# Attention scores in four column tiles of 32, masked in four pieces, with the value projection's scaling moved ahead of the third chunk's product

## The chip, the cores and the metric

The kernel runs on one core of a Trainium2 chip. The metric is the time on the device in microseconds, from several executions of which the median counts. One execution was profiled; all rows shown here are from that one.

A core has five engines that run side by side, each through its own queue in order: TensorE (PE, with its weight loads listed apart as PEld), VectorE (DVE), ScalarE (ACT), GpSimd (POOL) and SyncE (SP), which here only issues transfers.

## The reference

A layer of chunked linear attention, followed by a gated feed-forward layer, each with a residual and a layer normalization. Tokens are 4 x 2048 with 256 features. Cut to what matters:

```python
CHUNK = 32
Q, K, V = x @ W_q.T, x @ W_k.T, x @ W_v.T
diff = pos[:, None] - pos[None, :]                      # positions within a chunk of 32
mask = where(diff >= 0, decay ** diff, 0)
S = einsum('bncd,bnkd->bnck', Qc, Kc) * mask            # scores, 32 x 32 in each chunk
O = einsum('bnck,bnkd->bncd', S, Vc)
x = layernorm(x + (sigmoid(x @ W_g.T) * O) @ W_o.T + x)
gate = x @ (w_gate * SCALE).T                           # 768 hidden features
up = x @ (w_up * SCALE).T
x = layernorm(x + (silu(gate) * up) @ (w_down * SCALE).T)
```

Scores exist only inside a chunk of 32 tokens. Nothing passes from one chunk to the next.

## The kernel before

The 8192 tokens are worked through in 16 blocks of 512 (`TB`), each in four groups of 128 (`NG`). A token's features lie either along the partitions (`xT`, `yT`, `hT`) or along the free dimension (`x`, `v`, `h`, `r`). Query and key weights are multiplied into one matrix m beforehand, so that the scores of a block are products of xT with yT = m xT.

**Scores.** `attn_scores` takes a group of 128 tokens in two halves of 64 (`PAIR`, two chunks). Each half is a matmul with 64 stationary columns (tokens of xT) and 64 moving ones (of yT), over two slices of 128 features; every fp32 matmul is two instructions on PE. The result `ps`, 128 x 256 numbers, holds for each pair of chunks also the products between the two chunks, which are not wanted. One DVE multiply (L655) with `mask`, a constant tile of the same shape that is zero outside the chunks, writes `sT`. The tile `mask` is made at the start by four DVE copies (L274) from `chunk_mask`, a tile of 128 x 32 that holds the decay powers.

**Values.** `value_products` (L670) multiplies sT with v in 64 x 64 tiles, four at a time, into two banks `po`, and DVE makes `goT` of them with the gate `sg`.

**Split products.** The projections y (L494), gate g (L494), v and o (L516) are each made of three products of lower-precision parts: `hi`, `lo` and `gap`. `three` issues kinds hi and lo into two banks and lets ACT scale each bank (L535); the function that it returns issues the third kind, gap, and the bank's last use. The gap product therefore waits for ACT's scaling.

**Feed-forward, up.** `ffn_up` takes one of six chunks of 128 hidden features at a time: eight matmuls into banks `fg` and `fu` (L839), ACT's silu `s` (L848), DVE's product `u` (L859), ACT's rounding `u_hi` (L864) and POOL's remainder `u_lo` (L865). With `held=True` it returns a function `multiply` that issues u, u_hi and u_lo later. `ffn_down` is L710.

**The loop.** Iteration b of the main loop does the feed-forward of block b, the attention of block n = b + 2 and the projections of block m = b + 3. In program order: normalize h of block b + 1 (ACT, L428); up chunk 0; up chunk 1; move h of b + 1 (four DVE transposes into `sq`, L791, and 16 transfers on SP's queue into `hT`, L798); scores of block n; load xT of m + 1; up chunk 2; first two kinds of v for m with ACT's scaling; up chunk 3; the gap kind of v, normalization and store of a finished block; values of n; y of m and up chunks 4 and 5; split of hT (L815, L816); gate of m and output projection of n, with residual h and its statistics (L750, L340, L341); ACT's roots (L349); down. In the first iteration (b = 0) h of block 1 is normalized and moved only after the scores; the last one (b = 13) has no block m left and takes the scores after up chunk 0. Scores of blocks 0 and 1 are made ahead of the loop, those of block 1 between two residuals of block 0 (`beside`).

The order on PE, ACT and mostly DVE is the program's: `in_turn` and `in_steady_turn` pin an instruction to its place on its engine. What isn't pinned (POOL's remainders, transfers) may be placed elsewhere.

The PSUM has eight banks that all these products share. A further function, `wide_group`, treats weights of more than 8 bits; its branch isn't taken with these inputs.

Of the kernel before, what the change touches and what calls it, by code (L numbers as in the profile page):

```python
# [47 lines left out]
F32 = mybir.dt.float32  # L48
# [4 lines left out]
ALU = mybir.AluOpType  # L53

P = 128
CHUNK = 32
PAIR = 2 * CHUNK
SQ = 32
TB = 512
NG = TB // P  # L60
# [16 lines left out]
def kernel(  # L77
# [15 lines left out]
    nc = tc.nc  # L93
    NT, D = x.shape
    H = ffn_gT.shape[1]
    KD = D // P
    KH = H // P
    NB = NT // TB
# [15 lines left out]
    def in_turn(ins):  # L114
        tc.keep_in_program_order(ins)

    def bank(name):
        return psum.tile([P, TB], F32, tag="ps", name=name)
# [9 lines left out]
    def load_xT(b, start=None, pieces=1):  # L128
        xt = xin.tile([P, KD, TB], F32, tag="xT", name=f"xT_{b}")
        src = xT[:, span(b, start)].rearrange("(k p) t -> p k t", p=P)  # L130
        n = KD // pieces
        for k in range(0, KD, n):
            queue(start).dma_start(xt[:, k : k + n, :], src[:, k : k + n, :])
        return xt
# [106 lines left out]
    for i in range(CHUNK.bit_length() - 1):  # L241
# [10 lines left out]
        in_turn(nc.vector.tensor_copy(bit, bit_int))  # L252
        in_turn(nc.vector.tensor_scalar(factor, bit, -1.0, 1.0, ALU.mult, ALU.add))
        bits.append((bit, factor))
    mask = const.tile([P, NG, PAIR], F32, tag="mask", name="mask")
    nc.vector.memset(mask, 0.0)

    def make_mask():
        in_turn(nc.scalar.activation(decay, decay, AF.Sigmoid))
        power = decay  # L260
        for i, (bit, factor) in enumerate(bits):
            in_turn(
                nc.vector.scalar_tensor_tensor(factor, bit, power, factor, ALU.mult, ALU.add)
            )
            in_turn(nc.vector.tensor_tensor(chunk_mask, chunk_mask, factor, ALU.mult))
            if i < len(bits) - 1:
                square = const.tile([P, 1], F32, tag=f"power_{i}", name=f"power_{i}")
                in_turn(nc.vector.tensor_tensor(square, power, power, ALU.mult))
                power = square
        for g in range(P // CHUNK):  # L270
            rows = slice(g * CHUNK, (g + 1) * CHUNK)
            at = g * CHUNK % PAIR
            in_turn(
                nc.vector.tensor_copy(  # L274
                    mask[rows, :, at : at + CHUNK],
                    chunk_mask[rows, :].unsqueeze(1).to_broadcast([CHUNK, NG, CHUNK]),
                )
            )

    def integers(w, w_int, name):  # L280

# [46 lines left out]
    def in_steady_turn(ins):  # L328
        if steady:
            tc.keep_in_program_order(ins)  # L330
# [231 lines left out]
    def split_v(b, x_parts):  # L562
        v = work.tile([P, NG, D], F32, tag="v", name=f"v_{b}")
        per = TB // D

        def finish(i, pb):
            in_turn(nc.scalar.copy(flat(v, slice(i * per, (i + 1) * per)), pb))

        return v, three(f"v_{b}", token_major(w_parts["wv"], x_parts), finish)
# [67 lines left out]

    def attn_scores(b, yT):
        xt = xTs.pop(b)
        halves = [slice(i * PAIR, (i + 1) * PAIR) for i in range(P // PAIR)]  # L640
        ps = bank(f"ps_{b}")[:, : NG * PAIR].rearrange("p (g c) -> p g c", c=PAIR)
        for g in range(NG):
            for fc in range(KD):
                for rows in halves:
                    tokens = slice(g * P + rows.start, g * P + rows.stop)
                    product = nc.tensor.matmul(  # L646
                        ps[rows, g, :],
                        lhsT=xt[:, fc, tokens],
                        rhs=yT[:, fc, tokens],
                        start=(fc == 0),  # L650
                        stop=(fc == KD - 1),
                    )
                    in_turn(product)
        sT = work.tile([P, NG, PAIR], F32, tag="sT", name=f"sT_{b}")
        in_steady_turn(nc.vector.tensor_tensor(sT, ps, mask, ALU.mult))  # L655
        return sT

    def by_pairs(t):
        return t.rearrange("p k (g r c) -> p (k g) r c", g=NG, c=PAIR)
# [382 lines left out]
    def up_now(b, hT, uT, hc):  # L1042
        ffn_up(b, hT, uT, range(hc, hc + 1))

    for b in range(NB - 2):
        n = b + 2
        m = b + 3
        more = m < NB
        xns[n] = load_xn(n)
        hT = hTs.pop(b)  # L1050
        uT = [], []
        yT, v, sg = ahead
        if b:
            normalize(hs[b + 1], *scales_h)
        up_now(b, hT, uT, 0)
        if not more:
            sT = attn_scores(n, yT)
        up_now(b, hT, uT, 1)
        if b:
            moving = move_h(b + 1, hs[b + 1])  # L1060
        if more:
            sT = attn_scores(n, yT)
        if b == 0:
            normalize(hs[b + 1], *scales_h)
            moving = move_h(b + 1, hs[b + 1])
        if m + 1 < NB:
            xTs[m + 1] = load_xT(m + 1)
        up_now(b, hT, uT, 2)
        if more:
            v_next, v_rest = split_v(m, x_parts)  # L1070
            up_now(b, hT, uT, 3)
            v_rest()
            if scales_out is not None:
                normalize(r_before, *scales_out)
                store(b - 2, r_before)
        goT = attn_values(n, sT, v, sg)
        if b == 0:
            look_up(range(4, n_pieces))
            cast_fd(0)
        if b == 1:  # L1080
            count = count_wide()
            n_wide_early = const.tile([1, 1], I32, tag="n_wide_early", name="n_wide_early")
            nc.vector.tensor_copy(n_wide_early, count)
        go_parts, go_gaps = token_parts(goT, f"go_{n}")
        if more:
            y_next, y_rest = split_y(m, x_parts)
        else:
            up_now(b, hT, uT, 3)
            normalize(r_before, *scales_out)
            store(b - 2, r_before)  # L1090
        up_now(b, hT, uT, 4)
        go_gaps()
        up_now(b, hT, uT, 5)
        if b == 0:
            cast_fd(1)
        elif more:
            hTs[b + 1] = split_h(b + 1, moving)
        r_before = r_out
        if more:
            y_rest()  # L1100
            sg_next, g_rest = split_gate(m, x_parts)
            hs[n], out_rest = split_out(n, go_parts)
            g_rest()
            mv_h = out_rest()
            if b == 0:
                hTs[b + 1] = split_h(b + 1, moving)
            ahead = y_next, v_next, sg_next
            if m + 1 < NB:
                x_parts, x_gaps = token_parts(xTs[m + 1], f"x_{m + 1}")
            std_h = root_in_turn(mv_h, of_h, f"h_{b}")  # L1110
            if b:
                mv_before, std_before = mv_out, root_in_turn(mv_out, of_out, f"out_{b}")
            back_to_silu()

            def between():
                scales = scale_and_shift(mv_h, std_h, of_h, f"h_{b}")
                if m + 1 < NB:
                    x_gaps()
                return scales

            r_out, mv_out, scales_h = ffn_down(b, uT, hs.pop(b), between)
            if b:
                scales_out = scale_and_shift(mv_before, std_before, of_out, f"out_{b}")
        else:
            hs[n], out_rest = split_out(n, go_parts)
            hTs[b + 1] = split_h(b + 1, moving)
            scales_out = iterated_scale_and_shift(mv_out, of_out, f"out_{b}")
            normalize(r_before, *scales_out)
            store(b - 1, r_before)

            def amid():
                return iterated_scale_and_shift(out_rest(), (HALF, 1.0), f"h_{n}")

            r_out, mv_out, scales_h = ffn_down(
                b, uT, hs.pop(b), chunkwise=True, amid=amid
            )
            normalize(hs[n], *scales_h)
            scales_out = iterated_scale_and_shift(mv_out, of_out, f"out_{b + 1}")
# [164 lines left out]
    def wide_group(start, weights):  # L1303
# [11 lines left out]
        def products(pb, pairs):  # L1315
            for i, (lhsT, rhs) in enumerate(pairs):
                nc.tensor.matmul(
                    pb, lhsT=lhsT, rhs=rhs, start=(i == 0), stop=(i == len(pairs) - 1)
                )
            return pb  # L1320
# [25 lines left out]
            bank("pv_w")[:, :D], [(xt[:, ec, :], given["wv"][:, ec, :]) for ec in range(KD)]  # L1346
        )
        nc.vector.tensor_copy(v, pv)
        sT = work.tile([P, NG, PAIR], F32, tag="sT", name="sT_w")
        ps = bank("ps_w")[:, :PAIR]  # L1350
        for i in range(P // PAIR):
            rows = slice(i * PAIR, (i + 1) * PAIR)
            products(ps[rows, :], [(xt[:, fc, rows], yT[:, fc, rows]) for fc in range(KD)])
        nc.vector.tensor_tensor(sT[:, 0, :], ps, mask[:, 0, :], ALU.mult)
        banks = [
            bank(f"po_w_{i}")[:, :P].rearrange("p (n c) -> p n c", c=PAIR)
            for i in range(P // PAIR)
# [130 lines left out]
```

## Time and profile before

| | |
|---|---|
| time, median of 3 executions | 506.77 us (506.67 to 506.98) |
| the profiled execution's time | 507.07 us |
| its span, first to last instruction | 505.5 us |
| PE busy | 493.7 us, 98% |
| ACT, DVE, POOL busy | 373.1, 301.1 and 291.4 us |
| granted TensorE clock | 0.997 of full speed |
| ps (L646) | 512 matmul instructions, 16 groups of 1.08 us |
| sT (L655) | 16 DVE multiplies, median 385 ns |
| mask (L274) | 4 DVE copies, 1,218 to 1,259 ns |

A row of the profile names the line and engine, then the operation, then output and inputs by the program's tile names. Times within the span are counted from the first instruction. A row of a timeline begins with start and duration in us; in square brackets stands how long the engine stood idle before, and what ended that. A row of the waits reads: engine, tile and line that waited, what it waited for, then the total in us, how often, and the longest. Busy shares are averages: an engine at 60% can still be the one that a stage waits for.

### The profile page before, as it was taken

Reading aid. Unit: us, or ns where it says so; the run is one execution under the profiler, and the core shown is the slowest. Engines: PE = TensorE matmul, PEld = TensorE weight load, DVE = VectorE, ACT = ScalarE, POOL = GpSimd, SP = SyncE. Lnnn points to the kernel's source line nnn. Section 1 sums busy time; section 2 is a strip of 40 time slices with the busy share of each in tenths; the row PEclk is TensorE's granted clock in tenths of the full one; section 3 lists DMA queues with packets and bytes.
Section 4 is the critical chain, followed back from the end, with each engine's and each line's share of the span. In section 5 each row is a group of like instructions: output and inputs, shape, how many; then the busy total and the mean of one; then the engine's idle time right before and its main releaser. Section 6 shows DMA issues by size and latency. Waiting matters only on the chain.

```text
span 505.5 us, 11205 instructions
## 1 busy us (share of the span) xinstructions
PE 493.7 (98%) x4248; PEld 387.0 (77%) x4248; DVE 301.1 (60%) x709; ACT 373.1 (74%) x701; POOL 291.4 (58%) x322
## 2 busy tenths in 40 slices
PE   9999889999999999999999999999999999999995
PEld 5787667787777878777787877778787787867684
DVE  4887567564564647547464664747547463656654
ACT  5867777687768777686787868777786877766845
POOL 2745546654746557465564846557474655567664
PEclk9999999999999999999999999999999999999998
DMA  8721202112222122222212312122222211103111
GB/s 264 236 83 44 66 22 83 44 43 69 65 83 79 43 77 91 61 67 84 70 58 67 99 56 74 50 76 86 64 64 85 83 43 33 54 15 107 34 36 65
DMA packets 43320, 36.93 MB, mean 73 GB/s; under 512 B 4864, under 2 KB 39168, under 8 KB 43264
## 3 DMA queue, kind: packets, MB, share of 16 engines
q1 hardware_dynamic: 42144, 35.28, 23.4%
q10 hardware_dynamic: 1120, 0.92, 0.6%
q8 instruction: 34, 0.56, 0.5%
q14 instruction: 22, 0.18, 0.1%
HBM read 20.45 MB, written 8.39 MB: 57 GB/s over the span
## 4 chain that ended last, share of the span: by engine, by line
PE 69%; ACT 5%; DVE 4%; POOL 2%; SPq 2%; issue 2%; DMA 1%; DVEq 0%; ACTq 0%; POOLq 0%
PE fg L839 14%; PE fu L839 13%; PE fdn L710 12%; PE p_y L494 6%; PE p_g L494 6%; PE p_o L516 6%; PE p_v L516 6%; PE po L670 2%; PE ps L646 2%; DVE u L859 2%; SPq L798 2%; PE fdn L913 1%; ACT s L848 1%; ACT h L428 1%; ACT u_hi L864 1%
## 5 line engine op out<-in xcount | busy, mean ns | idle before, releaser
L865 POOL TENSOR_TENSOR u_lo<-u,u_hi 128x512 f16<-128x512 f32 (+1 forms) x98 | 128.9, 1317 | 94.1 <-ACT u_hi L864 94.1
L859 DVE SCALAR_TENSOR_TENSOR u<-fu,s 128x512 f32<-128x512 f32 (+1 forms) x98 | 66.4, 678 | 123.7 <-ACT s L848 98.3
L864 ACT CAST u_hi<-u 128x512 fp32r<-128x512 f32 (+1 forms) x98 | 59.9, 612 | 78.9 <-DVE u L859 78.8
L839 PE MATMUL fg<-hT_hi,fg_hi 128*128 128x512 f32 (+1 forms) x196 | 71.1, 444 | 0.0
L848 ACT ACTIVATE s<-fg 128x512 f32<-128x512 f32 (+1 forms) x98 | 56.8, 581 | 5.7 <-PE fg L839 5.5
L839 PE MATMUL fu<-hT_hi,fu_hi 128*128 128x512 f32 (+1 forms) x196 | 60.6, 390 | 0.0
L839 PE MATMUL fg<-hT_lo,fg_lo 128*128 128x512 f16 (+1 forms) x196 | 58.3, 378 | 0.0
L839 PE MATMUL fu<-hT_lo,fu_lo 128*128 128x512 f16 (+1 forms) x196 | 57.5, 375 | 0.0
L475 POOL TENSOR_TENSOR go_lo<-goT,go_hi 128x512 fp32r<-128x512 f32 x30 | 38.9, 1315 | 26.5 <-ACT go_hi L474 26.5
L475 POOL TENSOR_TENSOR x_lo<-xT,x_hi 128x512 fp32r<-128x512 f32 x30 | 38.3, 1299 | 23.8 <-ACT x_hi L474 23.8
L710 PE MATMUL fdn<-fd_hi,u_hi 128*128 128x256 f32 x312 | 44.8, 285 | 0.0
L750 DVE TENSOR_TENSOR h<-p_o,x 128x512 f32<-128x512 f32 x30 | 19.4, 686 | 41.9 <-PE p_o L516 37.6
L839 PEld LDWEIGHTS fu<-hT_hi,fu_hi 128*128 128x128 f32 x196 | 36.6, 188 | 8.4
L839 PEld LDWEIGHTS fg<-hT_hi,fg_hi 128*128 128x128 f32 x196 | 34.8, 189 | 9.4
L710 PEld LDWEIGHTS fdn<-fd_hi,u_hi 128*128 128x128 f32 x312 | 39.0, 188 | 0.3
L428 ACT ACTIVATE h<-h,shift_h,scale_h 128x256 f32<-128x256 f32 x52 | 27.0, 590 | 16.4 <-POOL shift_h L391 16.4
L710 PE MATMUL fdn<-fd_lo,u_lo 128*128 128x256 f16 x312 | 38.6, 274 | 0.0
L816 POOL TENSOR_TENSOR hT_lo<-hT,hT_hi 128x512 f16<-128x512 f32 x28 | 35.4, 1285 | 3.8 <-ACT hT_hi L815 3.7
L839 PEld LDWEIGHTS <-fu_lo 128*128 128x128 f16 x196 | 19.2, 98 | 22.3 <-issue 0.3
L710 PEld LDWEIGHTS <-u_lo 128*128 128x128 f16 x312 | 28.4, 98 | 3.9
L688 DVE SCALAR_TENSOR_TENSOR goT<-sg,po 128x512 f32<-128x512 f32 x32 | 20.6, 684 | 16.1 <-PE po L670 16.1
L839 PEld LDWEIGHTS <-fg_lo 128*128 128x128 f16 x196 | 14.0, 98 | 20.9 <-issue 12.9
(175 smaller groups left out, 1056.9 us busy)
## 6 DMA issues: line engine op xcount, KB each, us to landing
x<-in_x_dram SPq DMA_DIRECT2D x16, 512.0 KB, 3.9
xT<-in_xT_dram SPq DMA_DIRECT2D x15, 512.0 KB, 3.7
hT<-sq SPq DMA_DIRECT2D x224, 32.0 KB, 1.9
out_dram<-r SPq DMA_DIRECT2D x13, 512.0 KB, 3.1
out_dram<-r SPq DMA_DIRECT2D x7, 128.0 KB, 1.7
fg_int<-in_ffn_gT_dram SPq DMA_DIRECT2D x3, 256.0 KB, 7.8
fu_int<-in_ffn_uT_dram SPq DMA_DIRECT2D x3, 256.0 KB, 7.1
fd_int<-in_ffn_dT_dram SPq DMA_DIRECT2D x3, 256.0 KB, 5.9
```

The lines of the kernel that those rows point to most:

```text
L428: nc.scalar.activation(r[:, g, :], r[:, g, :], AF.Identity, bias=shift[:, g : g + 1], scale=scale[:, g : g + 1],)
L475: in_turn(nc.gpsimd.tensor_tensor(lo[:, k, :], t[:, k, :], whole, ALU.subtract))
L494: nc.tensor.matmul(pb, lhsT=a[kind][:, k, i * P : (i + 1) * P], rhs=b[kind][:, k, :], start=kind + k == 0, stop=True, skip_group_check=True,)
L516: nc.tensor.matmul(pb[:, j * D : (j + 1) * D], lhsT=b[kind][:, k, g * P : (g + 1) * P], rhs=a[kind][:, k, :], start=kind + k + j == 0, sto ...
L688: nc.vector.scalar_tensor_tensor(by_pairs(goT)[:, :, r, :], by_pairs(sg)[:, :, r, :], 1.0, po, ALU.add, ALU.mult)
L710: product = nc.tensor.matmul(pb[:, j * D : (j + 1) * D], lhsT=part[:, g * P : (g + 1) * P], rhs=w, start=(i == 0), stop=(i == len(terms) - 1),
L816: nc.gpsimd.tensor_tensor(in_order[1], whole, in_order[0].bitcast(F32), ALU.subtract)
L839: product = nc.tensor.matmul(pb, lhsT=w[kind][:, dc, hc * P : (hc + 1) * P], rhs=hT[kind][:, dc, cols], start=(kind == kinds[0] and dc == ...
L848: in_turn(nc.scalar.activation(s, pg, AF.Silu, scale=SCALE / H_UP))
L859: nc.vector.scalar_tensor_tensor(u, pu, U_UP / H_UP, s, ALU.mult, ALU.mult)
L864: in_steady_turn(nc.scalar.copy(hi, u))
L865: nc.gpsimd.tensor_tensor(lo, u, hi.bitcast(F32), ALU.subtract)
```

## The change

1. Scores are made chunk by chunk: four matmuls of 32 stationary columns and 32 moving ones, each in a column tile of its own (`tile_position`), so that only the wanted 32 x 32 products exist. `ps` is half as wide.
2. `mask` and its four copies go. Two constant tiles `sTs` are set to zero once on POOL and used in turn; each block multiplies its four chunks' rows with `chunk_mask` into the places of the tile that belong to them (four DVE instructions of 32 partitions x 128 elements). The rest stays zero.
3. In the loop, up chunk 2 is called with `held=True`, and its `multiply` stands behind the first two kinds of v, whose scalings on ACT thereby come ahead of u and u_hi of that chunk.
4. In the first iteration, normalizing and moving h of block 1 stand behind that `multiply`; the load of xT stands ahead of it.

```diff
-    mask = const.tile([P, NG, PAIR], F32, tag="mask", name="mask")
-    nc.vector.memset(mask, 0.0)
...
-        for g in range(P // CHUNK):
-            rows = slice(g * CHUNK, (g + 1) * CHUNK)
-            at = g * CHUNK % PAIR
-            in_turn(
-                nc.vector.tensor_copy(
-                    mask[rows, :, at : at + CHUNK],
-                    chunk_mask[rows, :].unsqueeze(1).to_broadcast([CHUNK, NG, CHUNK]),
-                )
-            )
+
+    sTs = [const.tile([P, NG, PAIR], F32, tag=f"sT_{i}", name=f"sT_{i}") for i in range(2)]
+    for sT in sTs:
+        nc.gpsimd.memset(sT, 0.0)
...
     def attn_scores(b, yT):
         xt = xTs.pop(b)
-        halves = [slice(i * PAIR, (i + 1) * PAIR) for i in range(P // PAIR)]
-        ps = bank(f"ps_{b}")[:, : NG * PAIR].rearrange("p (g c) -> p g c", c=PAIR)
+        ps = bank(f"ps_{b}")[:, : NG * CHUNK].rearrange("p (g c) -> p g c", c=CHUNK)
         for g in range(NG):
...
-        sT = work.tile([P, NG, PAIR], F32, tag="sT", name=f"sT_{b}")
-        in_steady_turn(nc.vector.tensor_tensor(sT, ps, mask, ALU.mult))
-        return sT
+            score_products(ps[:, g, :], xt[:, :, g * P :], yT[:, :, g * P :], in_turn)
+        sTs.append(sTs.pop(0))
+        masked(sTs[-1], ps, range(NG), in_steady_turn)
+        return sTs[-1]
+
+    chunks = [slice(i * CHUNK, (i + 1) * CHUNK) for i in range(P // CHUNK)]
+
+    def score_products(ps, xt, yT, order):
+        for fc in range(KD):
+            for chunk in chunks:
+                product = nc.tensor.matmul(
+                    ps[chunk, :],
+                    lhsT=xt[:, fc, chunk],
+                    rhs=yT[:, fc, chunk],
+                    start=(fc == 0),
+                    stop=(fc == KD - 1),
+                    tile_position=(0, chunk.start),
+                )
+                order(product)
+
+    def masked(sT, ps, groups, order):
+        for i, chunk in enumerate(chunks):
+            at = i * CHUNK % PAIR
+            order(
+                nc.vector.tensor_tensor(
+                    sT[chunk, groups.start : groups.stop, at : at + CHUNK],
+                    ps[chunk],
+                    chunk_mask[chunk, :].unsqueeze(1).to_broadcast([CHUNK, len(groups), CHUNK]),
+                    ALU.mult,
+                )
+            )
...
         if more:
             sT = attn_scores(n, yT)
+        if m + 1 < NB:
+            xTs[m + 1] = load_xT(m + 1)
+        multiply = ffn_up(b, hT, uT, range(2, 3), held=True)
+        if more:
+            v_next, v_rest = split_v(m, x_parts)
+        multiply()
         if b == 0:
             normalize(hs[b + 1], *scales_h)
             moving = move_h(b + 1, hs[b + 1])
-        if m + 1 < NB:
-            xTs[m + 1] = load_xT(m + 1)
-        up_now(b, hT, uT, 2)
         if more:
-            v_next, v_rest = split_v(m, x_parts)
             up_now(b, hT, uT, 3)
```

The branch for wide weights uses the same two functions; it isn't taken here.

## The prediction

> **What bounds the kernel now.** I read the page first (busy shares and the chain that ended last), then the chain in order of time, then the timelines of PE, ACT and DVE over one block of the steady loop.
>
> ```profile
> span 505.5 us, 11205 instructions
> PE 493.7 (98%) x4248; PEld 387.0 (77%) x4248; DVE 301.1 (60%) x709; ACT 373.1 (74%) x701; POOL 291.4 (58%) x322
> ...
> 205.49 1.08 PE ps L646 x32
> ...
> 235.57 1.08 PE ps L646 x32
> ```
>
> PE is busy 98% of the span, and from 145 to 444 us the chain runs on PE alone, with a period of 30.08 us (235.57 − 205.49). Each block holds one group of scores of 1.08 us. That looks like a plain PE bound, but the list of waits says otherwise:
>
> ```profile
> PEld p_g L494 <- ACT p_g L535: 4.2, 14, 1.5
> PEld p_o L516 <- ACT p_o L535: 2.2, 12, 0.2
> PE p_v L516 <- ACT p_v L535: 1.6, 1, 1.6
> ```
>
> In every block the weight loads of the last products of gate and output (third kind, "gap") wait for ACT's scaling of their banks. In the block at 205 the second scaling of p_o ends at 225.72 and its product starts at 225.87, 0.14 later; in the block at 114, where PE stood visibly idle at 134.07, that distance is also 0.14 (135.47 to 135.61). So PE and a second loop are level to some 0.02 us. The second loop: ACT normalizes h (202.80), s and u of chunks 0 and 1, DVE's four transposes, the masking, u of chunk 2, then ACT almost back to back to the scaling of p_o, PE's last p_o products, DVE's residual and statistics, ACT's roots, POOL's shift, and the next h at 232.88.
>
> ```profile
> 207.98 1.42 DVE L791 STREAM_TRANSPOSE sq<-h 128x256 f32<-128x256 f32 x4
> 209.32 0.39 DVE L655 TENSOR_TENSOR sT<-ps,mask 128x256 f32<-128x256 f32 x1
> 209.63 0.68 DVE L859 SCALAR_TENSOR_TENSOR u<-fu,s 128x512 f32<-128x512 f32 x1
> ...
> 210.34 0.62 ACT L864 CAST u_hi<-u 128x512 fp32r<-128x512 f32 x1 [1.12 <-DVE u L859]
> 210.86 1.06 ACT L535 ACTIVATE p_v<-p_v 128x512 f32<-128x512 f32 x2
> 211.90 0.60 ACT L848 ACTIVATE s<-fg 128x512 f32<-128x512 f32 x1
> ```
>
> Here ACT stands 1.12 us for u of the third chunk, with the scaling of p_v queued behind it. Both sides of the change touch this place.
>
> **What the skill says.** The Trainium skill, "TensorE: Matmul & The Clock Gate", section on packing small matmuls: matmuls of different tiles run at once, starting about 4 ns apart. The records of single matmuls agree in kind: the two 64-column tiles of ps start 7 ns apart and the pair repeats every 58 ns; po's four 64x64 tiles also start 7 ns apart and repeat every 58. The same page states a start-to-start floor of about 25 ns for small matmuls; po's 64 in 1.09 us (17 ns each) show that it can hold within one tile only. "TensorEngine Tiling (Array Packing)", key properties: changing the tiling mode drains TensorE; here the next full matmul starts 0.15 us after the last of ps. "VectorE: DVE Perf Modes", section on two Vector instructions with no wait between them: an instruction that starts in another quadrant of partitions is held until all earlier ones have finished. The four copies of L274 (32 partitions each) fit: each starts 14 ns after the end of the one before, while the transposes overlap by 78.
>
> **The change, part by part.**
>
> *PE, scores.* 64 matmuls of 32 columns in four tiles replace 32 of 64 in two: 16 rounds either way. A round is 58 ns; its streaming part follows from L599 (512 columns, 592 ns) and L620 (256 columns, 379): 0.83 ns a column, 53 for 64, 27 for 32. The new round is 32 ns, and issuing four pairs takes 4 x 7 = 28, just under it. Saved 16 x 26 = 0.42 us, group 1.08 to 0.66. Four streams at once on all 128 rows are not in this trace; bounds: nothing saved (rounds stay at 58), or 0.49 (issue alone). A loss would need 4 tiles to run one after the other, which po's four speak against. I take 0.42.
>
> *DVE, masking.* One multiply (385 ns, 416 unpipelined) becomes four of 32x128 in four quadrants. The PSUM read of nine numbers at L319 takes 148 ns, so 128 elements at one a cycle (the same page: 0.96 GHz, one a cycle for fp32 from PSUM) give about 272; from the 256-element row, 385 − 133 = 252 pipelined. The first starts pipelined with the transposes at 209.32, the others and u are held: u of chunk 2 starts near 209.32 + 0.25 + 3 x 0.29 = 210.45 instead of 209.63. Upper bound: L274's 1,234 ns a piece. Those copies keep step with POOL's 1.3 us operations beside them, whereas L655 took 390 ns under POOL's u_lo (208.80 to 210.10); so I keep 0.29, range 0.17 (overlapped) to 0.40.
>
> *ACT, order.* The scaling of p_v no longer stands behind u. s of chunk 2 ends at 209.22, p_v's first bank is ready by then with PE 0.42 earlier, the second is scaled 210.09 to 210.63, u is done at 210.45 + 0.69 = 211.14, u_hi starts 211.18, and s of chunk 3 at 211.70 instead of 211.90. The second loop is 0.20 shorter, PE's 0.42 shorter; the smaller counts: **0.20 a block, ten blocks (145 to 444 us), 2.0 us**. With pieces of 0.17 it is PE's 0.42; at 0.33 it is nothing.
>
> *First block of the loop (50 us).* Here h is normalized in front of chunk 2, and PE pays:
>
> ```profile
> 54.15 2.08 ACT L428 ACTIVATE h<-h,term_h,y_h 128x256 f32<-128x256 f32 x4
> ...
> 58.05 1.06 ACT L535 ACTIVATE p_v<-p_v 128x512 f32<-128x512 f32 x2
> ...
> 58.68 1.22 PE L516 MATMUL p_v<-wv_gap,x_gap 128*128 128x256 f32 x8 [1.62 <-ACT p_v L535]
> ```
>
> Now normalizing follows the scaling and u, so that idle goes. But ACT does the same work up to the gate scaling (72.0), where PE waits 1.3 us again. ACT gains only idle time: s 54.15, p_v 54.65 and 55.14, u_hi 55.65, h 56.15, s of chunk 3 at 58.1 instead of 59.04. Gain 0.94. The moves of h (four transposes, 16 DMAs on SP of 0.64 us) start 2.0 us later, their last landing goes from 68.7 to 70.8, still ahead of its reader at 74.9. The load of xT that now precedes them was issued ahead of them already (51.45).
>
> *Second block (84 us).* Its p_v wait (0.24) goes and the scores give 0.42; ACT is ahead of PE here by 0.9 in the gate: 0.66. *Third (114 us):* ACT waits 0.71 for h's transfer, one of whose pieces landed late (132.14). If that recurs nothing is gained, if not some 0.9: I take 0.45. *Last (444 us):* ACT waits 0.25 for chunk 1 behind the scores: 0.25.
>
> *Start.* Two score groups stand ahead of the loop, 0.84 on PE. The second is masked between residuals (DVE 34.15 to 34.57) and po starts at 34.85. With DVE 0.42 earlier and 1.15 of pieces, sT is ready at about 34.9, so PE waits what it gained: −0.1 in all. The removed mask copies (4.98 us at 11.63) and memset end ahead of yT, whose products PE finishes at 16.8: a few tenths at most, none of it counted. The two memsets on POOL fall in its idle 4.1 us before 6.29.
>
> Sum against the profiled execution: 0.94 − 0.1 + 0.66 + 0.45 + 2.0 + 0.25 = 4.2 of a span of 505.5 us. That execution took 507.07, 0.3 above the median 506.77; from the median: **502.5**.
>
> **Rivals.** *DVE is cheap* (pieces 0.17, not held): PE's 0.42 counts in ten blocks, 4.2, with 0.9 in the third; total 6.8, **500.0**. Against it are L274's gaps. *No saving on PE* (four streams share what two had): ten blocks 0, first 0.84, second 0.24, third 0.2; 1.3 in all, **505.5**. Nothing in this trace excludes it. *Masking is the bound, slower:* DVE between transposes and u of chunk 2. Above 0.33 us a piece the loop is longer than before, above about 0.40 the loss (3 us) exceeds all gains by over 1 us. At 0.46: u at 211.16, s at 212.41, +0.51 a block, 5.1 less 1.3 gained elsewhere, **510.5**; at L274's 1.25 it would be near 545. For it: the only row of this shape. Against: 385 ns for double the elements under the same POOL load. *Even:* 0.35 to 0.40 a piece, **506.5**.
>
> **Numbers.** Forecast 0.62, cheap DVE 0.13, no PE saving 0.11 (0.07 of it faster by more than 0.2%, 0.04 not), even 0.05, slower 0.09. A difference under 0.2% (1.0 us) is about what a measurement of this kernel can't tell from none. Faster 0.82, same 0.09, slower 0.09. The forecast's own range is 501 to 504; with the cheap-DVE case and the one without PE saving 499.8 to 505.7, leaving out the slow case and half of the even one.
>
> **What would show it.** Group of ps: x64 in some 0.66 us (right), 1.08 (rival two). sT: four pieces of about 0.27 us, each starting after the end of the one before. In steady blocks p_v scaled ahead of u_hi, ACT's idle before u_hi of chunk 2 gone, and a visible PE wait of about 0.2 us at the gate's or output's last products. At 58.7 no PE wait, at 72 a longer one. At 34 us a new wait of po for sT. A period of 29.9 us: 30.1 or more would make the loop's step wrong, 29.65 the DVE price.

## The result, and the profile after

The changed kernel took 502.51 us (median of 4 executions, 502.30 to 503.24), the kernel before 506.87 beside it (4 executions, 506.67 to 506.98): a ratio of 0.9917, interval 0.9900 to 0.9934. It is faster by 4.4 us. The prediction was 502.5.

The head of the page after and the chain of waits in order of time (start, duration, what):

```profile
span 500.8 us, 12278 instructions
PE 489.9 (98%) x4760; PEld 381.8 (76%) x4760; DVE 308.0 (61%) x752; ACT 373.4 (75%) x701; POOL 291.6 (58%) x324
```

```profile
201.60 0.69 PE ps L646 x50
...
231.53 0.69 PE ps L646 x50
```

The group of scores went from 1.08 to 0.69 us, although it is now 64 instructions. The period is 29.93 (231.53 − 201.60), where it was 30.08. PE is as busy as before, 98%: the busy share could not have told that the loop changed.

The list of waits (engine, tile and line that waited, releaser, total us, times, longest):

```profile
PEld p_g L486 <- ACT p_g L527: 6.3, 23, 1.7
PEld p_o L508 <- ACT p_o L527: 2.3, 12, 0.2
PE p_g L486 <- ACT p_g L527: 2.1, 3, 1.5
```

The visible wait of p_v (1.6 us before) is not in the list any more. The weight loads of the gate's last product wait longer than before (6.3 us against 4.2): PE now reaches that place too early. Why is in the timelines of DVE and ACT at the same place in the block (start, duration; idle before and its releaser in brackets):

```profile
204.09 1.42 DVE L803 STREAM_TRANSPOSE sq<-h 128x256 f32<-128x256 f32 x4
205.43 1.17 DVE L662 TENSOR_TENSOR sT<-ps,chunk_mask 32x128 f32<-32x128 f32 x4
206.63 0.69 DVE L871 SCALAR_TENSOR_TENSOR u<-fu,s 128x512 f32<-128x512 f32 x1
```

```profile
205.28 0.58 ACT L527 ACTIVATE p_v<-p_v 128x512 f32<-128x512 f32 x1
206.22 0.58 ACT L527 ACTIVATE p_v<-p_v 128x512 f32<-128x512 f32 x1 [0.36 <-PE p_v L508]
207.35 0.62 ACT L876 CAST u_hi<-u 128x512 fp32r<-128x512 f32 x1 [0.55 <-DVE u L871]
207.88 0.59 ACT L860 ACTIVATE s<-fg 128x512 f32<-128x512 f32 x1
```

Masking takes 1.17 us instead of 0.39, and u begins 2.54 us behind the first transpose (206.63 − 204.09) instead of 1.65 (209.63 − 207.98): 0.89 later. ACT used that time for p_v's scaling, but still stood 0.55 us for u. The silu s of the fourth chunk follows the start of h's normalization by 8.97 us (198.91 to 207.88); before it was 9.10 (202.80 to 211.90). Those 0.13 us are the gain of an undisturbed block.

### The profile page after: what moved, and what is told of

It reads as the page before. It is cut to its first block, busy times and chain, and to the rows that moved or that the text cites. A ratio compares the mean times of both kernels' runs of the same rounds, so it can differ in the third digit from the quotient of the medians.

```text
span 500.8 us, 12278 instructions
## 1 busy us (share of the span) xinstructions
PE 489.9 (98%) x4760; PEld 381.8 (76%) x4760; DVE 308.0 (61%) x752; ACT 373.4 (75%) x701; POOL 291.6 (58%) x324
## 4 chain that ended last, share of the span: by engine, by line
PE 81%; ACT 8%; DVE 7%; issue 2%; POOL 1%; DVEq 0%; ACTq 0%; POOLq 0%
PE fg L851 15%; PE fu L851 14%; PE fdn L722 12%; PE p_v L508 8%; PE p_y L486 8%; PE p_g L486 7%; PE p_o L508 6%; PE po L682 3%; DVE u L871 3%; PE ps L646 2%; ACT s L860 1%; ACT r L420 1%; PE fdn L925 1%; PE pi L193 1%; PE pa L722 1%
```

## The experiments

The change has three parts that can be had singly: the four tiles, the cutting of the mask, and the order of the loop. Theory: the loop has two closed chains of nearly equal length, PE's own work and the chain through ACT and DVE; the tiles shorten the first, the order the second, and the pieces lengthen the second again. Rivals: PE alone bounds the loop (it was 98% busy), or something else holds it at 29.95.

Each kernel is timed against the kernel before in its own series: 506.87 us for the changed one, 507.46 for the next four (10 executions), 507.50 for the last three (9). So the ratios can be compared across the table, the times only within a series. "Period" is the median of the nine distances between normalizations of h from 142 to 414 us before and the same nine blocks elsewhere; "start" runs from the first scores to those of the first iteration, "first" from there to those of the second iteration, all in the profiled execution. As a median, the period leaves out single longer blocks.

| kernel | us | ratio (interval) | period | start | first |
|---|---|---|---|---|---|
| before | 506.87 | 1 | 30.08 | 29.73 | 33.58 |
| changed | 502.51 | 0.9917 (0.9900 to 0.9934) | 29.95 | 29.66 | 31.60 |
| order_only | 504.91 | 0.9951 (0.9934 to 0.9967) | 30.10 | 29.73 | 31.75 |
| pieces_old_order | 518.03 | 1.0209 (1.0192 to 1.0226) | 30.95 | 29.66 | 34.10 |
| whole_old_order | 506.08 | 0.9967 (0.9955 to 0.9979) | 30.03 | 28.94 | 33.57 |
| whole_new_order | 499.58 | 0.9841 (0.9825 to 0.9858) | 29.72 | 28.95 | 31.60 |
| pieces_by_group | 499.37 | 0.9836 (0.9822 to 0.9851) | 29.74 | 28.95 | 31.58 |
| pieces_behind_u | 500.14 | 0.9859 (0.9844 to 0.9874) | 29.74 | 29.66 | 31.59 |
| after_wide_late | 504.94 | 0.9943 (0.9930 to 0.9957) | 29.96 | 29.63 | 34.25 |

### order_only: the new order alone

The kernel before, with parts 3 and 4 of the change:

```diff
+        if m + 1 < NB:
+            xTs[m + 1] = load_xT(m + 1)
+        multiply = ffn_up(b, hT, uT, range(2, 3), held=True)
+        if more:
+            v_next, v_rest = split_v(m, x_parts)
+        multiply()
         if b == 0:
             normalize(hs[b + 1], *scales_h)
...
-        up_now(b, hT, uT, 2)
-            v_next, v_rest = split_v(m, x_parts)
```

> The kernel before with the new order of the loop alone: scores in 64-column tiles and one masking multiply as before (group of ps 1.08 us, sT 0.39 us). Theory (PE and a loop over ACT and DVE are level in the steady blocks): the loop over ACT gets shorter by some 0.6 us, PE not at all, so the period stays near 30.07 us; gained are 1.9 us in the first block, 0.24 in the second and some 0.4 in the third; 504.3 us. Rival (the change's gain came from the order, everywhere): about 502.5 as with the whole change. Rival (it came from PE's shorter groups alone): no gain, 506.9.

504.91 us. The period did not move (30.10 against 30.08); the first iteration is shorter by 1.83 us. The order shortens the chain of ACT and DVE alone, and PE does not follow: all that it gains by itself lies ahead of the steady loop.

### pieces_old_order: four tiles and four pieces, in the old order

The changed kernel with parts 3 and 4 taken back (the same lines the other way round).

> The change without its new order: four-tile scores and masking in four pieces, but the scaling of p_v behind u of the third chunk, and h of block 1 normalized ahead of the third chunk. Theory: masking takes 1.20 instead of 0.31 us of the way from DVE's transposes to u, and p_v's scaling and s of chunk 3 are behind it, so the loop over ACT is 0.9 us longer and PE waits: period near 30.95 us, ten blocks 8.9 us, less about 0.6 elsewhere; 515 us. Rival (masking on DVE is off the path): PE's 0.39 us a group counts, 500.7 to 502.

518.03 us, slower than before by 2.1%. ACT in the same place:

```profile
215.38 0.62 ACT L876 CAST u_hi<-u 128x512 fp32r<-128x512 f32 x1 [2.02 <-DVE u L871]
215.90 1.06 ACT L527 ACTIVATE p_v<-p_v 128x512 f32<-128x512 f32 x2
```

The wait for u of the third chunk went from 1.12 to 2.02 us, and p_v's scaling stands behind it. The period is 0.87 us longer, near 9 us in ten blocks, for a step that saves PE 0.39 each. The time is 3 us above what was expected. 0.6 is the series (507.46 for the kernel before, not 506.87). In the profiled execution the first scores come 1.0 us later than before (21.50 against 20.48), and the first iteration is 0.5 us longer (34.10); both touch PE's clock, told in the last section.

### whole_old_order and whole_new_order: four tiles, one multiply

`ps` stays at 32 columns per group, and one DVE multiply reads each of them twice, once for each half of `sT`, against the old tile `mask`, whose zeros clear the unwanted half. The first in the old order, the second in the new.

```diff
-        in_steady_turn(nc.vector.tensor_tensor(sT, ps, mask, ALU.mult))
+    def twice(t):
+        return t.rearrange("p g (r c) -> p g r c", c=CHUNK)
...
+            nc.vector.tensor_tensor(
+                twice(sT[:, groups, :]),
+                ps.unsqueeze(2).to_broadcast([P, n, PAIR // CHUNK, CHUNK]),
+                twice(mask[:, groups, :]),
+                ALU.mult,
+            )
```

> Old order, four-tile scores, but the masking as one multiply: the old 128x256 mask stays, and the 32 columns of ps are read twice (broadcast), so that one DVE instruction of some 0.39 us writes sT, zeros included. PE's group is 0.69 us. Theory (two loops level): the loop over ACT and DVE is as long as before, so PE's 0.39 us turns into waiting: period 30.0 to 30.1; gained are some 0.6 in front of the loop, 0.4 in the second block and 0.28 in the last; 505.4 us. Rival (PE alone bounds the steady blocks): 0.39 x 16 = 6.2, 500.6 us.

> As the run before with the new order: one multiply of some 0.39 us for the masking, p_v's scaling ahead of u. Theory (in the changed kernel the four pieces on DVE hold the loop, 0.25 us a block short of what PE could give): u of the third chunk comes 0.9 us earlier, s of the fourth waits for PE, PE's 0.39 us counts in full: period near 29.7 us, 2.5 us less than the changed kernel in the loop and some 0.7 less in front of it, where po no longer waits for the masking; 499 us (498 to 500). Rival (something else, like the landing of h, holds the loop at 29.95): 501.8 us.

506.08 and 499.58 us. With the old order PE's saving is nearly all turned into waiting (period 30.03). The weight loads of the gate from 140 to 435 us, in the kernel before and in whole_old_order:

```profile
PEld p_g L494 <- ACT p_g L535: 1.5, 9, 0.2
PEld p_g L494 <- ACT p_g L535: 4.0, 19, 0.3
```

With the new order it counts almost in full: 29.72, the old period less 0.36, of 0.39 saved. The waits of PE's weight loads in the same stretch, ten blocks, of the changed kernel first and then of whole_new_order:

```profile
PEld p_g L486 <- ACT p_g L527: 4.1, 19, 0.5
PEld p_o L508 <- ACT p_o L527: 1.9, 10, 0.2
```

```profile
PEld p_o L516 <- ACT p_o L535: 1.9, 10, 0.2
PEld p_g L494 <- ACT p_g L535: 1.8, 11, 0.2
```

The output's wait is the same. The gate's differs by 2.3 us, 0.23 a block, which is near the distance of the two periods (29.95 and 29.72). Near only: in the two kernels below with a period of 29.74 it is 0.5 and 1.3 us, so this sum gives the direction better than the size. The rivals fall by the periods: neither step alone moves the period by more than 0.05 where both together move it by 0.36, which a PE bound does not do, and nothing else holds the loop at 29.95. Masking with one multiply also keeps 0.7 us ahead of the loop (column "start").

### pieces_by_group: four pieces again, cut the other way

whole_new_order, with its multiply split by token group, so that every piece covers all partitions:

```diff
-        masked(sT, ps, in_steady_turn)
+        for g in range(NG):
+            masked(sT, ps[:, g : g + 1, :], in_steady_turn, slice(g, g + 1))
```

> Scores in 32-column tiles, the new loop order, and the masking in four multiplies again, but cut by token group: each takes 128 partitions x 64 elements instead of 32 x 128. The elements written are the same 256 per partition as in the single multiply. Theory (a piece is dear because it changes the quadrant of partitions and is held for the one before): these four begin in the same quadrant and overlap, some 0.2 us each and about 0.1 apart; u of the third chunk comes about 0.2 us later than with the single multiply, which p_v's second scaling covers, so the period stays PE's 29.7 us and the time is that of whole_new_order, 499.6 (499 to 500.5). Rival (four instructions cost what they cost however they are cut): pieces of about 0.3 us one after the other, a period of 29.95 as in the changed kernel, 502 to 502.5.

499.37 us, period 29.74: as with one multiply. DVE's timeline:

```profile
205.77 0.58 DVE L668 TENSOR_TENSOR sT<-ps,mask 128x64 f32<-128x64 f32 x4
206.27 0.67 DVE L877 SCALAR_TENSOR_TENSOR u<-fu,s 128x512 f32<-128x512 f32 x1
```

Four instructions in 0.58 us, each of 184 to 208 ns and begun 0.11 to 0.13 us after the one before, where four that change their quadrant (a group of 32 partitions) take 1.17. It is not the number of instructions that costs. Here each piece, and u behind them, starts 0.08 us before the end of the one ahead; in the changed kernel pieces 2 to 4 and u start 0.01 to 0.03 us after it. The Trainium skill, "VectorE: DVE Perf Modes", section on two Vector instructions with no wait between them, says that an instruction starting in another quadrant than the last is held until all earlier ones have finished; both timelines agree. The two kinds of piece differ in length too, 64 elements per partition here and 128 there, twice as many in all. How much of the 0.59 us between 0.58 and 1.17 is the holding and how much the length, no run separates.

### pieces_behind_u: the same pieces, elsewhere on DVE

The changed kernel, with the pieces of the loop issued behind u of the third chunk:

```diff
-            sT = attn_scores(n, yT)
+            sT = attn_scores(n, yT, later)
...
         multiply()
+        for mask_now in later:
+            mask_now()
```

> The changed kernel, with the four masking pieces of each block in the loop issued behind u of the third chunk on DVE instead of ahead of it. The work of DVE is the same. Theory (the pieces cost time only because u of the third chunk, and with it ACT's s of the fourth, stand behind them): u follows the transposes, the period is PE's 29.7 us as in whole_new_order, 0.25 less than the changed kernel in ten blocks; the 0.8 us that the pieces cost ahead of the loop remain; 500.0 to 500.5. Rival (DVE's added 0.7 us a block count wherever they stand, by what comes behind them): a period of 29.95, 502 to 502.5. A second rival: sT comes too late for its products; then slower than the changed kernel.

500.14 us, period 29.74, with DVE as busy as in the changed kernel (307.3 and 308.0 us):

```profile
204.94 0.68 DVE L875 SCALAR_TENSOR_TENSOR u<-fu,s 128x512 f32<-128x512 f32 x1
205.53 1.20 DVE L666 TENSOR_TENSOR sT<-ps,chunk_mask 32x128 f32<-32x128 f32 x4
```

The pieces cost the loop nothing once u stands ahead of them; it was their place, not their work. The 0.7 us at the start remain. That is about the distance to whole_new_order (0.6 us), though the intervals of the two overlap.

### after_wide_late: one operation of the first iteration put back

DVE's comparison `wide<-top` is not pinned to a place. In the kernel before it stood behind go_gap and ahead of u of chunk 5; in the changed one it stands ahead of u of chunk 4. This kernel is the changed one with the comparison pinned to its old place:

```diff
-        nc.vector.tensor_scalar(wide, top, EXACT, None, ALU.is_gt)
...
+        if b == 0:
+            in_turn(nc.vector.tensor_scalar(wide, top, EXACT, None, ALU.is_gt))
```

> The changed kernel, with the one unpinned comparison of DVE (wide<-top, 1.27 us in the first block) put back to the place that it had in the kernel before, behind the gap product's split and ahead of u of chunk 5, instead of ahead of u of chunk 4. Theory (the first block of the loop gained 1.0 us more than forecast because this operation left ACT's path to the gate's scaling): the first block is 1.0 us longer, 503.5 (503.2 to 503.8). Rival (the gain came from p_v's wait and the order alone): 502.5 as the changed kernel.

504.94 us, above the 503.2 to 503.8 that were expected; 0.6 of that is the series again. By the ratios that is 0.0026 more than the changed kernel, 1.3 us, which the intervals (0.9900 to 0.9934 and 0.9930 to 0.9957) allow from near zero to 2.9. The traces carry the cause. First the changed kernel's DVE, then this one's:

```profile
63.72 0.92 DVE L305 TENSOR_SCALAR wide<-top 128x9 f32<-128x9 f32 x1
...
67.26 0.69 DVE L871 SCALAR_TENSOR_TENSOR u<-fu,s 128x512 f32<-128x512 f32 x1
```

```profile
67.31 1.26 DVE L1108 TENSOR_SCALAR wide<-top 128x9 f32<-128x9 f32 x1
68.49 0.68 DVE L871 SCALAR_TENSOR_TENSOR u<-fu,s 128x512 f32<-128x512 f32 x1
```

u of chunk 5 starts 1.23 us later, and the first gate scaling ends 21.45 us behind the scores of that iteration instead of 20.40: 1.05 later, as the theory gave. The rest of the longer first iteration in this execution (34.25 against 31.60) is PE's clock, told in the last section. The comparison stands early (63.6 to 64.4) in every other kernel with the new order, and late (68.0 to 69.4) in the three with the old one: it was the new order that moved it.

## Why the prediction was right, step by step

The span fell by 4.8 us (505.53 to 500.76), 4.2 was the sum. That the total came out so near is luck in good part: the ten steady blocks, the main term, gave 1.2 us less than forecast, the first and the third block 1.5 more. By the trace, cut at the scores of the first iteration and from there at the normalizations of h:

| part | predicted | measured |
|---|---|---|
| start | −0.1 | −0.04 |
| first block | 0.94 | 1.95 |
| second block | 0.66 | 0.79 |
| third block | 0.45 | 0.92 |
| ten steady blocks | 2.0 | 0.80 |
| last block and end | 0.25 | 0.35 |

**Scores on PE: right.** 0.69 us against 0.66, so 0.39 saved against 0.42. The rival that four streams share what two had is excluded.

**Masking on DVE: right in kind, a little small.** The pieces are held one behind the other, as foreseen. Their starts in the block above are 0.25, 0.31, 0.30 apart and u's is 0.33 behind the last piece's, in all 1.20 us; the prediction had 0.25 + 3 × 0.29 = 1.12. It knew the pause of 14 ns behind a held instruction and did not put it into the sum; the pauses were 13 to 32 ns.

**A steady block: mechanism right, size off.** This is the step that was mis-sized: 0.20 forecast, 0.13 measured in an undisturbed block. The missing 0.07 is about the 0.08 by which the pieces were longer than priced. That u stands between the two loops and that the smaller of the savings counts is shown by the experiments; with cheap pieces the period is 29.72 to 29.74, where 29.65 was forecast. PE's forecast wait of about 0.2 us a block is there, mostly on its weight loads: the gate's waited 4.1 us in ten blocks instead of 1.5, which is 0.26 a block, what PE saves (0.39) less what the block gains (0.13). One of the signs did not come true: ACT's idle ahead of u_hi of the third chunk was to be gone, and 0.55 us are left. The prediction's own times had this gap, from 210.63 to 211.18.

Ten blocks at 0.13 would be 1.3. The other 0.5 lies in single blocks: two of the nine periods after were 30.30 us, one of those before 30.32. In each of the two after, DVE pauses once, and the profile shows nothing that it waited for:

```profile
307.57 0.69 DVE L871 SCALAR_TENSOR_TENSOR u<-fu,s 128x512 f32<-128x512 f32 x1 [0.39 <-issue]
...
375.87 0.69 DVE L905 SCALAR_TENSOR_TENSOR r<-fdn,h 128x512 f32<-128x512 f32 x1 [0.25 <-issue]
```

The same two pauses, at the same two of DVE's 752 instructions, are in pieces_old_order, pieces_behind_u and after_wide_late, and in no kernel without the four pieces by quadrant. So they belong to the program and not to the execution; what DVE does in them is open. The transfer of h is not the cause: in this profile ACT waits for it only at 98.51 (0.51 us) and 457.58 (0.82), outside the ten blocks.

**First block: right in part, and 1.0 us short.** The PE wait for p_v at 58.68 went and one at the gate's product took its place, as the prediction said:

```profile
56.56 1.10 PE L508 MATMUL p_v<-wv_gap,x_gap 128*128 128x256 f32 x8
...
70.70 1.21 PE L486 MATMUL p_g<-x_gap,wg_gap 128*128 128x512 f32 x4 [1.49 <-ACT p_g L527]
```

But the step "ACT does the same work up to the gate scaling" took all of ACT's idle time up to there as fixed except 0.94. Part of that idle was u of chunk 5 standing behind `wide<-top` on DVE, and that operation, pinned to nothing, was placed elsewhere in the new program. The profile before had shown it, as 1.86 us of idle ahead of ACT's u_hi, ended by DVE's u; after, 0.81 are left:

```profile
69.92 0.62 ACT L864 CAST u_hi<-u 128x512 fp32r<-128x512 f32 x1 [1.86 <-DVE u L859]
...
67.98 0.62 ACT L876 CAST u_hi<-u 128x512 fp32r<-128x512 f32 x1 [0.81 <-DVE u L871]
```

after_wide_late puts the operation back, and 1.05 us return with it.

**Third block: luck.** The prediction took the middle of two outcomes, and the good one came: the late piece of h's transfer did not recur; that block lasted 29.95 instead of 30.87.

**Start: right.** The new wait of po for sT is there, and of the 0.8 us that PE saves in two groups nearly nothing is left behind it (29.66 us against 29.73):

```profile
34.59 0.33 PE L682 MATMUL po<-sT,v 64*64 64x64 f32 x4 [0.34 <-DVE sT L662]
35.13 1.15 PE L682 MATMUL po<-sT,v 64*64 64x64 f32 x60 [0.20 <-DVE sT L662]
```

With a single multiply the start is 0.7 us shorter, so this loss belongs to the pieces.

**The rival on the slow side** was the right danger with the wrong price: in the old order the same pieces make the kernel 2.1% slower. Only the order, which puts p_v's scaling into the time that they take, turns the sign.

## What to carry to other kernels

- Where two chains of a loop are level, shortening one gives nothing and a change has to be judged as a pair: the order alone moved the period by 0.02 us, the tiles with one multiply alone by 0.05, both by 0.36. Look for the wait that grows on the engine that was made faster.
- What splitting a Vector operation costs depends on how it is cut, not on the number of pieces alone: four pieces of 64 elements over all partitions took 0.58 us, four of 128 elements in different quadrants 1.17, one whole 0.39. Where the pieces stand matters as much: behind u the same four cost the loop nothing that its period shows. An operand that is read twice by a broadcast can spare the split altogether; that gave the best kernels here, 499.4 to 499.6 us.
- An operation that is pinned to no place may move when the program around it changes. List those that stand on the path, since a gain or a loss of 1 us can come from them alone.

## What the runs showed of the hardware

**PE's clock is set in steps of 3.41 us, and halves after a step with enough idle time.** In after_wide_late PE stood 2.51 us for the gate's scaling (69.40 to 71.91). From 1.2 us after it resumed, matmuls of 256 columns followed each other at 213 ns instead of some 115. The table by stretch (bounds, length, busy time and count of each engine, granted clock, DMA share, GB/s):

```profile
69.00:72.00 3.00, 0.49 (x5) 0.29 (x3) 1.36 (x3) 2.80 (x6) 1.27 (x1) 1.00 0.11 28
72.00:72.90 0.90, 0.90 (x4) 0.53 (x5) 0.00 (x0) 0.90 (x3) 0.00 (x0) 1.00 0.00 0
72.90:76.40 3.50, 3.50 (x18) 3.28 (x18) 2.14 (x5) 3.48 (x8) 1.51 (x2) 0.52 0.00 0
76.40:80.00 3.60, 3.60 (x33) 3.32 (x32) 2.75 (x10) 3.06 (x4) 3.48 (x3) 0.99 0.49 150
```

A clock of 0.52 over 3.5 us is 1.7 us of PE time, the rest of that first iteration's loss. pieces_old_order shows the same from 60.90 to 64.31 us (clock 0.50) behind an idle of 1.99 us. whole_old_order had an idle of 1.99 us too and kept its clock.

The traces record when the granted clock changes. In after_wide_late it is full from 4.80 us, half from 73.07, and full from 76.48 to 499.73: 20, 1 and 124 steps of 3.413 us. In all nine traces the stretches at full clock are such multiples. Laid over PE's idle time, these steps sort the cases. The step ahead of the slow one held 2.25 us of idle in after_wide_late (69.65 to 73.07) and 1.99 in pieces_old_order (57.48 to 60.90). The 1.99 us of whole_old_order fell on two steps, 0.97 ahead of 58.26 and 1.02 behind it. In the kernel before, 1.62 us in one step (55.43 to 58.84) left the clock as it was. So in these traces the limit lies between 1.62 and 1.99 us of idle in one step, about half of it. The steps begin at another place in each of these executions, so the same wait of 2 us can cost 1.7 us more or nothing.

The Trainium skill, "TensorE: Matmul & The Clock Gate", section on what is actually happening, tells of this gate with a window of about 3.4 us that runs freely, and the steps agree. It puts the drop after at least one idle window; here a window that was idle for little more than half was enough. The mean clock of the profiled execution of after_wide_late was 0.993, and 0.996 to 0.998 in the four others of this kernel, whose spans were 0.3 to 1.0 us shorter; how often the drop happens can't be read from that.

**The same clock sets the start.** Full clock is granted from 4.23 us in the kernel before, from 4.45 in the changed one and only from 7.13 in whole_new_order. PE's first matmuls show it (before, then whole_new_order):

```profile
4.62 3.60 PE L578 MATMUL pg<-xT,wg 128*128 128x512 f32 x8
4.97 4.67 PE L578 MATMUL pg<-xT,wg 128*128 128x512 f32 x8
```

At half clock the 2.90 us between cost 1.45, and the first scores start at 21.92 instead of 20.48. The table's columns leave this stretch out; the times contain it, so that single executions can differ by up to 1.4 us without the kernel.

**A stride of zero on a PSUM operand cost nothing here.** The multiply that reads `ps` twice took 385 ns, as the one that read 256 separate numbers.

**Four column tiles reach 10.8 ns a matmul instruction.** 64 instructions of 32 columns took 0.69 us up to the next product, where 32 of 64 columns had taken 1.08.
